# Five of the sixteen steps of L1F get other places in the schedule

## The chip, the cores and the metric

The kernel runs as one program on one core of a Trainium2 chip. The core has five engines, each with an instruction queue of its own that it works off in order: PE (matrix products), DVE (vector work), ACT (activation functions and copies), POOL (more vector work) and SP (issues DMAs). They meet only through semaphores. The metric is the time of the program on the device in microseconds (us).

## The reference

The network has four layers, L0 to L3. Each layer is a half-weighted feed-forward part, an attention and the same feed-forward part again, each applied to the layer-normed activations and added to them. `x` is 8 batches of 512 tokens by 128 features, f32. The change touches only L1's feed-forward part, called L1F here:

```
cluster_idx = argmax(calibrate(xf @ cluster_sigs.T))           # 8 clusters
tile_gates  = calibrate(xf @ sigs.T)                           # 64 tiles, 8 to a cluster
local_idx   = argmax(tile_gates of the chosen cluster)
comp = tanh(gelu(xf @ w1 + b1) @ w2 + b2)                      # 2 values a token
hh   = relu(comp @ spline_w1[tile] + spline_b1[tile])          # 16 values
mag  = hh @ spline_w2[tile] + spline_b2[tile]
y    = xf + mag * directions[tile] * output_scale
out  = layernorm(y) * gamma + beta
```

`calibrate` is a sigmoid, a place among 8 knots, a look-up of the knot's value and slope, and a line between them. L1's attention has 16 heads of 8 features over 512 tokens: scores, softmax, weighted sum, output product.

## The kernel before

`l0_block` does L0; `l0_tail` ends it and begins L1F; `l1_block` holds L1's attention with most of both L1F rounds beside it; `l2_block` and `l3_block` do the rest. What follows is about `l1_block`, which takes some 413 to 985 us of the profile.

**Units.** `l1_block` walks 128 units, (batch b, head group g, token tile i), 16 to a batch. In the text, u0 to u15 are the units of such a sixteen and block B is units 16B to 16B+15. Unit n issues, in two halves, `first(n)` (two matmuls a half, line 1290, into one of two PSUM buffers `s1`; then one DVE maximum over that buffer, line 1291, 128x2 out of 128x1024) and, 11 units late, `second(n-11)` (two matmuls a half, line 1310, with exponentials on ACT, line 1312). So PE can be at most one unit ahead of the maxima: the scores of a half wait for the maximum of the same half one unit before. After the two halves come the "works" planned for the unit, then, in every fourth unit, `weigh` (line 1320: 16 matmuls, 32 PE instructions), then the work of the dictionary `later`: the transposes `turn` (line 1330) with a reciprocal and a product on DVE (lines 1332, 1333), `back`, `leave`, and `maxima` (line 1298). With the lag of 11, `weigh` falls into u3, u7, u11 and u15. All PSUM tiles other than `s1` share one ring of four banks, `s2`: the scores of `second`, `o` of `weigh`, `tp` of `turn`, `pa`, `pp` and so on.

PE, ACT and DVE run in exactly the order in which the Python code issues (`manual_schedule`); POOL and SP are not in that list; the framework orders their instructions.

**The plan.** `todo` maps a slot to works; unit n carries out slots 2n and 2n+1. `plan` puts the steps of one L1F round of batch b at slots 32b + L1F_PLACES[k], for b = 2 to 7 and, for the second round, for two more with 32*8 and 32*9 in place of 32b:

```
L1F_PLACES = (-63, -58, -58, -55, -50, -50, -48, -47, -42, -42, -39, -37, -34, -31, -26, -22)
...
if b >= 2:
    self.plan(todo, [n + k for k in L1F_PLACES], *self.l1_ffn_steps(b, w, bank, room, self.xn[b], self.xt[b], aside=True))
```

Places repeat after 32 slots, so slot -63 is in u0, -58 in u3, -42 in u11, -31 in u0 of the next block, and so on. Eight rounds go through: their first halves (steps 1 to 13) lie in blocks 0 to 7, their last three steps one block later.

**The sixteen steps** (`l1_ffn_steps`):

```
steps = [lambda: powers(kept[:, :, 0:8]), places, lookup, gates, lambda: first("oc"), pick, lambda: powers(box["sg"]), places, lookup,
         gates, outer, turn, spline, direct, lambda: (whiten or self.whiten)(b, box["z"], box["z"]), update]
```

`powers` is one exponential on ACT (line 1081). `places` is five DVE operations on 128x32 (1087 to 1091). `lookup` is two DVE products of two SBUF operands (1096, 1097). `gates` is a DVE sum over the knots (1102) and two small DVE `tensor_tensor`, g (1104, 1105). `first` is five small DVE operations, the choice of a cluster (1111 to 1115). `pick` is a DVE product and a sum (1119, 1120). `outer` is a second choice and a product (1126). `turn` and `spline` go through PE, ACT and DVE (1131 to 1155). `direct` makes z on PE, ACT and POOL (1163, 1167). The norm, `whiten`, is four `bn_stats` on DVE (215), thirteen small POOL operations (219 to 236) and four POOL `tensor_scalar` (275). `update` is three POOL `tensor_tensor` on 128x512 (1173, 1175, 1176).

**What else is planned there.** For each next batch: a norm of x (`whiten`) at u7, its transposes on PE (line 314) at u9, the projections (1242, with rotation on POOL, 1246 and 1251) at u10 and u11, `values` at u12. In blocks 5 and 6 the front of a second L1F round comes on top (norm u15, transposes u2, scores and squeeze u3, its end u6). In block 7 the first steps of L2 take the place of the next batch's.

Of the kernel before, what the change touches and what calls it, by code (L numbers as in the profile page):

```python
# [70 lines left out]
values ffn1_13 squeeze6_1 clear11 ffn1_14 squeeze7_2 spread02 spread03 spread00 squeeze6_2 spread01  # L71
"""

L1F_PLACES = (-63, -58, -58, -55, -50, -50, -48, -47, -42, -42, -39, -37, -34, -31, -26, -22)
FIXED = {mybir.EngineType.PE, mybir.EngineType.Activation, mybir.EngineType.DVE}

ROWS = ["l0_bc", "l1_bo", "gamma", "beta", "l2_bo", "l3_bv"]
# [67 lines left out]
class Net:  # L145
# [1037 lines left out]
    def l1_block(self, w, w2, room, pool_w):  # L1183
# [18 lines left out]
        with ExitStack() as c:  # L1202
# [160 lines left out]
            for b in range(NB):  # L1363
# [5 lines left out]
                if b >= 2:  # L1369
                    self.plan(todo, [n + k for k in L1F_PLACES], *self.l1_ffn_steps(b, w, bank, room, self.xn[b], self.xt[b], aside=True))  # L1370
            for b in range(2):
                n = 32 * (NB + b)
                self.plan(todo, (n - 98, n - 91, n - 89, n - 89, n - 83), lambda _, b=b: self.whiten(b, self.xn[b]),
                          lambda xn, b=b: self.turned(xn, bank, self.xt[b]), *self.l1_ffn_front(b, w, bank, room))
                self.plan(todo, [n + k for k in L1F_PLACES], *self.l1_ffn_steps(b, w, bank, room, self.xn[b], self.xt[b], aside=True))
            n = 32 * NB - 50 + 32
# [713 lines left out]
```

## Time and profile before

| what | value |
|---|---|
| runs | 2604.12, 2608.65, 2613.46 us, median 2608.65 |
| the profiled execution | 2601.68 us, its span 2599.8 us |
| busy: PE, DVE, ACT, POOL | 91%, 78%, 68%, 44% of the span |
| granted PE clock, block 0 (417 to 484 us) | 0.75 |
| granted PE clock, blocks 1 to 6 (484 to 875 us) | 1.00 |
| length of blocks 0 to 7, us | 66.6, 63.8, 64.6, 64.5, 64.6, 67.2, 67.2, 59.1 |

The length of a block is the distance between the first line-1290 matmuls of its unit 0 and of the next block's. Within block 4, which starts at 676.53 us, the units last, from u0 to u15: 4.76, 2.45, 2.45, 5.77, 2.52, 3.72, 2.45, 5.77, 2.95, 4.18, 3.84, 7.41, 3.45, 4.00, 2.46, 6.41 us.

How to read the views: a timeline row gives the start, the time taken, the engine, the line of the code, the operation, output and inputs by the program's names, and how many instructions were merged (x6); in square brackets stands the idle time of the engine before it and who ended it. A row of the chain of waits gives start, length, engine, tile and line of the work that the end of the program was traced back through. In a group row, the numbers after the first bar are the time busy and the mean in ns of one instruction, after the second the idle time before them and what ended most of it.

### The profile page before, as it was taken

To read this page: it belongs to the slowest core of one execution; us is meant where nothing else is said; L and a number is where in the kernel's file an instruction comes from. 1 tells how busy PE (TensorE), PEld (TensorE's weight loads), DVE (VectorE), ACT (ScalarE), POOL (GpSimd) and SP (SyncE) were. 2 spreads that over 40 slices of the span, in tenths; PEclk is the share of its full clock that TensorE was granted. 3 is DMA by queue.
4 is the path that set the end of the run, shared out by engine and by line. 5 is a ranking of instruction groups with operands and counts; after the bars stand their busy time and mean duration, and the time that the engine had idled before them with its cause. 6 is when DMAs were issued, how large, how long until landed. Compare 5 with 4: busy or idle time off the path is not lost.

```text
span 2599.8 us, 51330 instructions
## 1 busy us (share of the span) xinstructions
PE 2375.4 (91%) x18184; PEld 1421.3 (55%) x18184; DVE 2019.7 (78%) x5582; ACT 1761.3 (68%) x4413; POOL 1154.4 (44%) x2016
## 2 busy tenths in 40 slices
PE   6868938999999998999999999999899999999997
PEld 6546623344444344565555655656565666666664
DVE  5356368888888847878878787876788989898897
ACT  2244233666677666866767667676688998999996
POOL 5754751444454332264352634432234545454443
PEclk9978957999999999999999999999899999999999
DMA  8221330001010100000000000000000000000000
GB/s 272 59 79 42 107 97 1 19 19 27 20 26 19 35 2 4 1 1 1 1 1 1 1 1 1 1 1 17 1 18 15 5 22 22 10 14 22 22 2 13
DMA packets 72976, 66.51 MB, mean 26 GB/s; under 512 B 15690, under 2 KB 62802, under 8 KB 70578
## 3 DMA queue, kind: packets, MB, share of 16 engines
q1 hardware_dynamic: 68112, 54.88, 7.8%
q0 software_dynamic: 3584, 7.58, 1.1%
q8 instruction: 145, 2.38, 0.4%
q10 hardware_dynamic: 1026, 0.78, 0.1%
q14 instruction: 109, 0.89, 0.1%
HBM read 36.47 MB, written 26.80 MB: 24 GB/s over the span
## 4 chain that ended last, share of the span: by engine, by line
PE 63%; DVE 21%; ACT 8%; POOL 4%; issue 2%; DMA 1%; SPq 0%; ACTq 0%; DVEq 0%; POOLq 0%
PE tp L1477 8%; PE s L1451 6%; PE s L1290 5%; PE o L1804 4%; PE o L1493 4%; PE o L1320 4%; PE s L1753 4%; PE yp L384 3%; PE s L1310 3%; ACT e L1760 3%; DVE nm L1291 3%; DVE nm L1455 3%; PE tp L1779 2%; PE pp L1721 2%; PE hp L684 2%
## 5 line engine op out<-in xcount | busy, mean ns | idle before, releaser
L1462 ACT ACTIVATE e<-s,nm 128x512 f32<-128x512 f32 x512 | 345.0, 688 | 25.9 <-DVE nm L1455 21.4
L1291 DVE TENSOR_REDUCE nm<-s 128x2 f32<-128x1024 f32 x256 | 301.3, 1218 | 75.8 <-PE s L1310 60.9
L1455 DVE TENSOR_REDUCE nm<-s 128x2 f32<-128x1024 f32 x256 | 300.9, 1216 | 29.8 <-PE s L1451 27.8
L1483 ACT ACTIVATE p<-tp 128x512 f32<-128x512 f32 x512 | 278.7, 617 | 63.8 <-PE tp L1477 63.8
L1312 ACT ACTIVATE pr<-s 128x512 f32<-128x512 f32 x512 | 271.5, 601 | 73.1 <-PE s L1310 69.5
L1477 PE MATMUL tp<-cst,e 128*128 128x128 f32 x2048 | 292.8, 281 | 15.2 <-DVE rs L1468 7.9
L1477 PEld LDWEIGHTS tp<-cst,e 128*128 128x128 f32 x2048 | 220.1, 141 | 153.7 <-issue 87.4
L1471 POOL TENSOR_SCALAR e<-e,rs 128x512 f32<-128x512 f32 x113 | 198.3, 1755 | 230.0 <-DVE rs L1468 191.5
L1290 PE MATMUL s<-k,q 32*128 32x512 f32 x1024 | 279.4, 658 | 18.0 <-DVE nm L1291 14.7
L1310 PE MATMUL s<-q,k 32*128 32x512 f32 x1024 | 290.3, 627 | 5.4 <-DVE at L1333 4.3
L1760 ACT ACTIVATE e<-e,m 128x512 f32<-128x512 f32 (+3 forms) x512 | 286.3, 571 | 12.7 <-DVE m L1757 12.5
L1757 DVE CUSTOM_DVE_ANT_0 e<-s,bias 128x512 f32<-128x512 f32 (+3 forms) x512 | 220.1, 486 | 93.2 <-PE s L1753 92.7
L219 POOL TENSOR_TENSOR d<-st 128x4 f32<-128x4 f32 (+3 forms) x90 | 19.5, 217 | 549.4 <-DVE st L215 351.3
L1781 ACT COPY pt<-tp 128x512 f32<-128x512 f32 x320 | 174.4, 589 | 90.3 <-PE tp L1779 90.2
L1471 DVE TENSOR_SCALAR e<-e,rs 128x512 f32<-128x512 f32 x399 | 195.6, 520 | 9.1
L1790 DVE TENSOR_SCALAR e<-e,rc 128x512 f32<-128x512 f32 (+3 forms) x512 | 190.0, 416 | 9.1
L386 DVE SCALAR_TENSOR_TENSOR x<-yp,sel,x 128x128 f32<-128x128 f32 x480 | 166.8, 348 | 32.4 <-PE yp L384 20.9
L1779 PE MATMUL tp<-cst,e 128*128 128x128 f32 x1280 | 171.0, 278 | 9.8 <-ACT pt L1781 4.0
L1451 PE MATMUL s<-k,q 32*128 32x512 f32 x1024 | 174.7, 651 | 5.1 <-ACT e L1462 2.6
L1753 PE MATMUL s<-qk 64*128 64x512 f32 (+3 forms) x1024 | 173.4, 457 | 2.0 <-DVE m L1757 1.3
L1493 PE MATMUL o<-p,va 128*32 128x128 f32 x4096 | 165.8, 277 | 2.9 <-ACT p L1483 2.9
L1779 PEld LDWEIGHTS tp<-cst,e 128*128 128x128 f32 x1280 | 139.2, 141 | 48.5 <-issue 13.6
(476 smaller groups left out, 4844.7 us busy)
## 6 DMA issues: line engine op xcount, KB each, us to landing
yd<-z SPq DMA_DIRECT2D x8, 1024.0 KB
r<-yd SPq DMA_DIRECT2D x32, 256.0 KB
sk<-pu SPq DMA_DIRECT2D x16, 256.0 KB
k<-sk SPq DMA_DIRECT2D x60, 64.0 KB
w<-in_l_w SPq DMA_DIRECT2D x14, 256.0 KB
xd<-wqkv SPq DMA_DIRECT2D x12, 256.0 KB
x<-in_x SPq DMA_DIRECT2D x8, 256.0 KB
up<-in_l_up SPq DMA_DIRECT2D x8, 256.0 KB
```

Of the source, the lines that this page charges most:

```text
L1290: nc.tensor.matmul(s[:, jj, :], lhsT=q[cut, g, i * P : (i + 1) * P], rhs=k[cut, g, :], start=True, stop=True)
L1291: nc.vector.tensor_reduce(nms[b, g // 2][:, i, 2 * h : 2 * h + 2, g % 2], s, AX.X, ALU.max, negate=True)
L1310: nc.tensor.matmul(s, lhsT=k[cut, g, kt * P : (kt + 1) * P], rhs=q[cut, g, :], start=True, stop=True)
L1451: nc.tensor.matmul(s[:, jj, :], lhsT=q[cut, g, i * P : (i + 1) * P], rhs=k[cut, g, :], start=True, stop=True)
L1455: nc.vector.tensor_reduce(nm, scores[n, h], AX.X, ALU.max, negate=True)
L1462: nc.scalar.activation(e, s[:, jj, :], AF.Exp, bias=nm[:, jj : jj + 1], accum_out=sm[:, jj : jj + 1])
L1471: (nc.gpsimd if h and jj and 14 <= n < last - 1 else nc.vector).tensor_scalar(e, e, rc[:, jj : jj + 1], None, ALU.mult)
L1477: nc.tensor.transpose(tp[:, kt, :], probs[n][j][:, kt * P : (kt + 1) * P], self.ident)
L1483: nc.scalar.activation(p, turns[n].pop(0), AF.Exp)
L1753: nc.tensor.matmul(s[:, jj, 0:w], lhsT=qs[n][cut, i * P : (i + 1) * P], rhs=ks[n][cut, 0:w], start=True, stop=True)
L1760: outs.append(lambda e=e, jj=jj: nc.scalar.activation(e, e, AF.Exp, bias=mins[n][:, jj, i : i + 1], scale=-1.0, accum_out=sums[n][:, jj, i ...
L1779: nc.tensor.transpose(tp[:, k, :], block(n, jj, i, kt), self.ident)
```

## The change

Only the tuple of places differs:

```diff
-L1F_PLACES = (-63, -58, -58, -55, -50, -50, -48, -47, -42, -42, -39, -37, -34, -31, -26, -22)
+L1F_PLACES = (-63, -61, -58, -55, -53, -51, -48, -47, -44, -42, -39, -37, -34, -31, -27, -22)
```

In units of a block this moves five steps:

| step | unit before | unit after |
|---|---|---|
| `places`, first round (step 2) | u3, ahead of `lookup` | u1 |
| `first("oc")` (step 5) | u7, ahead of `pick` | u5 |
| `pick` (step 6) | u7 | u6 |
| `lookup`, second round (step 9) | u11, ahead of `gates` | u10 |
| last norm, `whiten` of z (step 15) | u3, ahead of the next round's `places` | u2 |

No instruction is added or taken away, and L2's attention, which has a list of places of its own in `l2_block`, stays as it is. `places`, `first`, `pick` and `lookup` consist of DVE instructions alone; the norm is DVE and POOL.

## Prediction

> **What bounds the kernel.** I read the page's group list first. The maxima of L1's scores are the DVE's largest group there, and what ends the DVE's idle time before them is PE:
>
> ```profile
> L1291 DVE TENSOR_REDUCE nm<-s 128x2 f32<-128x1024 f32 x256 | 301.3, 1218 | 75.8 <-PE s L1310 60.9
> ```
>
> So in most places the DVE waits for PE. Next, the chain of waits through block 4 (676 to 742 us) shows where it is the other way round:
>
> ```profile
> 682.48 1.22 DVE nm L1291
> ...
> 688.47 3.57 PE o L1320 x32
> ...
> 695.50 0.54 DVE kd L1102
> ```
>
> The chain passes from PE to the maxima in u1 (682.48), is PE's alone in `weigh` (688.47 in u3, again at 702.93, 721.32 and 737.64), and in u4 goes through the DVE's `gates` (695.50). An ordinary unit is DVE-bound: PE needs 1.93 us for its scores (676.53 to 678.46 in u0), the two maxima need 2.42, the unit lasts 2.45. A `weigh` unit has 3.57 us more on PE, and DVE work planned there is under that cover. How much of the cover is used shows in the timeline of the DVE:
>
> ```profile
> 658.31 0.53 DVE L1104 TENSOR_TENSOR g<-t,kd 128x32 f32<-128x32 f32 x1
> 658.88 1.20 DVE L1105 TENSOR_TENSOR g<-g,kd 128x32 f32<-128x32 f32 x1
> ...
> 682.46 7.27 DVE L1291 TENSOR_REDUCE nm<-s 128x2 f32<-128x1024 f32 x6 [0.76 <-PE s L1310]
> ...
> 692.00 0.62 DVE L1097 TENSOR_TENSOR pr<-eq,tab 128x448 f32<-128x448 f32 x1
> 693.14 2.35 DVE L1291 TENSOR_REDUCE nm<-s 128x2 f32<-128x1024 f32 x2 [0.52 <-PE s L1310]
> ...
> 696.06 0.24 DVE L1104 TENSOR_TENSOR g<-t,kd 128x32 f32<-128x32 f32 x1
> ...
> 696.94 7.25 DVE L1291 TENSOR_REDUCE nm<-s 128x2 f32<-128x1024 f32 x6
> ```
>
> The six maxima of u1 to u3 run without a gap from 682.46 (the row's idle time of 0.76 is before the first). Norm, `places` and `lookup` follow, end at 692.62, and the DVE then still idles 0.52 us: in u3 all of them are free. From 696.94 the six of u5 to u7 run without a gap too, and the first two rows show the same two products g as at 696.06, but much longer. POOL's timeline says why:
>
> ```profile
> 657.51 2.52 POOL L1246 TENSOR_TENSOR rt<-rt,rope 128x512 f32<-128x512 f32 x2 [0.80 <-ACT rt L1245]
> ...
> 690.59 0.20 POOL L219 TENSOR_TENSOR d<-st 128x4 f32<-128x4 f32 x1 [8.38 <-DVE e L1087]
> ...
> 695.02 3.14 POOL L275 TENSOR_SCALAR z<-z,sm,rs 128x128 f32<-128x128 f32 x4
> 698.25 1.27 POOL L1173 TENSOR_TENSOR z<-z,gh 128x512 f32<-128x512 f32 x1
> ...
> 700.93 1.26 POOL L1176 TENSOR_TENSOR x<-x,z 128x512 f32<-128x512 f32 x1
> ```
>
> Beside a pair of POOL's 128x512 `tensor_tensor` (657.51 to 660.03) the g's took 0.53 and 1.20 us, each to about the end of one of the two. Beside POOL's `tensor_scalar` (695.02 to 698.16) they took 0.24 and 0.19. So the former block a DVE product of two SBUF tiles, the latter hardly do.
>
> **The change, part by part** (times of block 4; what is added to a unit's DVE queue always stands behind its own maxima and ahead of the next unit's, for which PE waits).
>
> *`places`, u3 to u1.* Five DVE operations, 1.13 us from the first's start to the next maximum (454.61 to 455.74 in block 0). In u1 they stand ahead of the maxima of u2; PE's u3 scores wait for those, and `weigh` is queued behind them: it began at 688.40, 1.10 after the last maximum of u2. Two pairs of maxima that no longer follow directly win a little back (six take 7.27, a spacing of 1.21; a pair alone 2.36, a spacing of 1.14): 1.13 - 2 x 0.07 = **1.0 us late**. Nothing returns in u3, whose DVE queue had already been free. In blocks 5 and 6 PE's own transposes (750.55) lengthen u2 to 2.79 and take 0.3 of it: 0.7.
>
> *The last norm, u3 to u2.* Its 0.78 us on the DVE (689.64 to 690.42) now stand ahead of u3's maxima. PE's next use of those is u4, behind `weigh`'s 3.57 us: nothing. z has been there since 682.20. But POOL starts earlier, and here is a new wait. u2's maxima end at 688.3, `bn_stats` at 689.1, and POOL's run begins at 689.15. From its begin to the first 128x512 operation it took 7.66 us in this block (690.59 to 698.25) and 7.07 with nothing beside it (741.17 to 748.24, an earlier part of block 5). So POOL's three-operation `update` starts at 696.2 to 697.0 and lasts 4 us; before, it lay under the maxima of u5 and u6, which read PSUM (their 1.21 is unchanged there). u4's maxima start at 693.14 + 1.0, `gates` 2.27 later, its g's at 697.05: inside POOL's first operation. Each waits for one POOL operation's end, at 697.5 to 698.3 and 698.85 to 699.6, where they would have ended at 697.5. That is 1.3 to 2.1, and 1.7 is the middle; the rows at 658.31 and 658.88 cost 1.3 in the same situation, by 0.29 and 1.01. Bounds: 0 if POOL misses them altogether, 2.4 if both wait for a whole 1.26 less their slack. I take **1.7 us**, the worked-out position. Behind the g's stand u4's `at` (line 1333), for which PE already waits in u5 (a bank of `s2`: matmul at 697.17, idle 0.38), and u5's maxima, so all of it is late.
>
> The Trainium skill weighs here, in "SBUF — State Buffer", section "Who interferes with whom": a DVE instruction with two SBUF inputs blocks against any GpSimd instruction that reads SBUF. By it the `tensor_scalar` at 695.02 would have held the g's too, some 1.3 us that the profile does not show (0.24 and 0.19); the move would then cost only about 0.4 a block here, and the whole sum would be about 14 us. I go by the rows.
>
> *`first`, u7 to u5.* 1.11 us (704.89 to 706.00) ahead of u6's maxima, less 0.14 as above: u5 to u7 are DVE-bound, `weigh` of u7 comes **1.0 late**. *`pick`, u7 to u6.* 1.03 us ahead of u7's maxima, covered by `weigh` as the norm was. What is late next: the norm of x in u7 now stands behind `pick` instead of before both, so relative to PE POOL starts it 0.9 later; its last tile came at 712.25, the last transpose of it at 713.36, a slack of 1.1. Just covered: nothing, but 0.5 to 0.9 in six blocks if POOL is slower.
>
> *Second `lookup`, u11 to u10.* 1.35 us (720.85 to 722.27 less a gap) go into 1.49 us of idle DVE before u11's maxima (716 to 718.58). In u11 `gates` ends up to 2.8 earlier, clear of POOL's rotation, but the DVE idled 1.30 before the maxima of u12 already, waiting for PE behind `weigh`. Nothing in blocks 1 to 7.
>
> *Two blocks differ.* In block 0 PE runs no `second` until u11; u6 and u7 begin with DVE idle times of 1.04 and 1.05, which take `first` and `pick`, and u9 waits for POOL either way (457.66). In u11, though, the maxima at 469.82 start straight behind a 1.19 us g; without it PE is ready at about 467.7 to 468.6. I put down **-1.3** (0 to -2). In block 7 the transposes of u9 wait for POOL (tile at 913.25, transpose at 913.31; u9 lasts 5.25 against 4.0 to 4.2), and there `first` and `pick` had stood ahead of the norm; the same wait shrinks by **1.2**. After unit 128 there are no maxima, and the norm's move is off the path.
>
> **Sum.** Blocks 1 to 4: 4 x (1.0 + 1.7 + 1.0) = 14.8. Blocks 5 and 6: 2 x (0.7 + 1.7 + 1.0) = 6.8. Block 7: 3.7 - 1.2 = 2.5. Block 0: -1.3. Together +22.8 us, all between 417 and 935 us. Against the profiled execution (2601.68, of which 2599.8 span) that is 2624.5; it was 7 us quicker than the median of the runs, 2608.65, and measured times are medians, so I forecast 2608.65 + 22.8 = **2631.5 us**.
>
> **The rivals.** (1) POOL's `update` misses `gates`: 7 x 1.7 less, +10.9, 2619.5. For it: a POOL run 0.4 longer than worked out lets the first g through. Against: then the second g, or `first` at about 700.3, meets the rest of its 4 us. (2) The x norm comes too late for u9, or both g's pay 2.4: 5 us each, up to +33, 2641.5. For it: a slack of 0.2 after the shift; against: in blocks 5 and 6 the slack was 1.6. (3) Faster: POOL's hold on the g's of u11 sets the start of u12. Moving `lookup` frees the DVE 2.8 us sooner there, and if u12's maxima had waited for it they would gain what block 0 gains, 1.3 in each of eight blocks; with `places` and `first` absorbed by the 0.5 us that PE is idle in a bare unit this gives -10, 2598. It decides from the point where the DVE's end in u11 is later than PE's scores of u12. Against: the DVE had 1.30 to spare. (4) The path does not move: PE's gaps of 0.46 and 0.18 in u2 and u3 take the shifts, 2608.65. Against: the gaps are waits for the very maxima that come later.
>
> **Numbers.** Forecast 0.57, rival 1 0.21, rival 2 0.11, rival 3 0.06, rival 4 0.05. About 0.3%, 7.8 us, is what a measurement here can tell from no change. Faster 0.06; within it 0.07 (rival 4 and the lower edge of rival 1); slower 0.87. The range, 2614 to 2642, spans rivals 1 and 2 with some microseconds of spread between runs (2604 to 2613 before), and leaves out the faster case and no change.
>
> **What would show it.** Block 4 should last 68.3 us instead of 64.6; u3's `weigh` begins 1.0 later within its block; the DVE's g's in u4 take around 0.5 to 1.2 each; u6 and u7 show `first` and `pick` between maxima; the DVE idles some 2 us in u3 and u7 before the next maxima, unused cover. If u4's g's stay at 0.2, rival 1 holds. If blocks 1 to 4 are no longer than before, the reading of the cover is wrong.

## The result, and the profile after

Medians of six runs each: 2608.73 us before (2604.12 to 2613.46), 2623.39 us after (2620.27 to 2630.36). The ratio is 1.0063, 95% interval 1.0051 to 1.0076: 13.3 to 19.8 us slower, 14.7 by the medians. The profiled execution took 2627.5 us, of which 2625.5 span.

| length, us | 0 | 1 | 2 | 3 | 4 | 5 | 6 | 7 | sum |
|---|---|---|---|---|---|---|---|---|---|
| blocks before | 66.63 | 63.79 | 64.61 | 64.46 | 64.61 | 67.15 | 67.17 | 59.09 | 517.5 |
| blocks after | 65.24 | 67.79 | 66.95 | 66.82 | 67.44 | 71.39 | 70.28 | 60.86 | 536.8 |
| difference | -1.39 | +4.00 | +2.34 | +2.36 | +2.83 | +4.24 | +3.11 | +1.77 | +19.3 |

Block 7 is counted here to the first scores of its u15. The profile shows 25.8 us more for the whole execution, 19.3 of it in the blocks. The rest is 0.3 before L1, 5.9 between the last score of L1 (line 1290) and the first of L2 (line 1753), and 0.3 after that. The 5.9 are a matter of their own, further below. The profiled execution of before was 7 us quicker than its median and this one 4 us slower, so the profiles differ by more than the medians.

The group of the maxima is as busy as it was (301.3 us) and the DVE's idle time before it grew from 75.8 to 101.8 us. The moved work left its old places empty:

```profile
L1291 DVE TENSOR_REDUCE nm<-s 128x2 f32<-128x1024 f32 x256 | 301.3, 1217 | 101.8 <-PE s L1310 88.9
```

The chain of waits in block 4 (from 684.11 us on), which answers to the chain shown of before:

```profile
696.99 3.57 PE o L1320 x32
...
704.02 0.54 DVE kd L1102
704.58 0.77 DVE g L1104
706.20 1.09 PE s L1310 x2
```

u3's `weigh` now starts 12.88 us into the block (696.99) where it started 11.94 into it (688.47). New on the chain is the product g (704.58). Behind it on the DVE stands `at` (line 1333), for which PE waits with the scores of `second` (706.20; idle 0.89 where it had been 0.38). The DVE's timeline of the same stretch says what happened in each unit:

```profile
692.32 0.17 DVE L1087 TENSOR_SCALAR e<-e 128x32 f32<-128x32 f32 x1
...
693.45 2.35 DVE L1291 TENSOR_REDUCE nm<-s 128x2 f32<-128x1024 f32 x2
...
701.67 2.35 DVE L1291 TENSOR_REDUCE nm<-s 128x2 f32<-128x1024 f32 x2 [1.88 <-PE s L1310]
...
704.58 0.76 DVE L1104 TENSOR_TENSOR g<-t,kd 128x32 f32<-128x32 f32 x1
705.37 0.19 DVE L1105 TENSOR_TENSOR g<-g,kd 128x32 f32<-128x32 f32 x1
...
718.08 2.35 DVE L1291 TENSOR_REDUCE nm<-s 128x2 f32<-128x1024 f32 x2 [1.85 <-PE s L1310]
```

`places` (from 692.32) pushes the maxima of u2 back to 693.45, by 1.13. In u3 and u7 the DVE now idles 1.88 and 1.85 us under `weigh`: unused cover. Of the two g's the first is held (0.76 where it had been 0.24) and the second is not (0.19). POOL's timeline has the holder:

```profile
700.80 3.14 POOL L275 TENSOR_SCALAR z<-z,sm,rs 128x128 f32<-128x128 f32 x4
704.02 1.27 POOL L1173 TENSOR_TENSOR z<-z,gh 128x512 f32<-128x512 f32 x1
705.37 1.32 POOL L1175 TENSOR_TENSOR z<-z,gh 128x512 f32<-128x512 f32 x1
```

The first g ends at 705.34, POOL's first operation at 705.29. The second g runs at the boundary to POOL's next, which starts at 705.37 and takes 1.32 in place of 1.27. So it was in blocks 2, 3, 4 and 7, and in block 6, where the first g took 1.03. In blocks 1 and 5 the second g was held too and took 1.30, and u5 is 1.1 longer there than in the neighbours (5.34 against 4.23, 4.87 against 3.75).

### The profile page after: what moved, and what is told of

Read it like the earlier page. It is cut to its first block, busy times and chain, and to the rows that moved or that the text cites. A ratio compares the mean times of both kernels' runs of the same rounds, so it can differ in the third digit from the quotient of the medians.

```text
span 2625.5 us, 51330 instructions
## 1 busy us (share of the span) xinstructions
PE 2382.8 (91%) x18184; PEld 1421.6 (54%) x18184; DVE 2014.3 (77%) x5582; ACT 1760.8 (67%) x4413; POOL 1154.8 (44%) x2016
## 4 chain that ended last, share of the span: by engine, by line
PE 62%; DVE 22%; ACT 8%; POOL 4%; issue 2%; DMA 1%; SPq 0%; ACTq 0%; DVEq 0%; POOLq 0%
PE tp L1477 8%; PE s L1451 6%; PE s L1290 5%; PE o L1320 4%; PE o L1493 4%; PE o L1804 4%; DVE nm L1291 4%; PE s L1753 4%; PE yp L384 3%; PE s L1310 3%; ACT e L1760 3%; DVE nm L1455 3%; PE tp L1779 2%; PE pp L1721 2%; PE hp L684 2%
## 5 line engine op out<-in xcount | busy, mean ns | idle before, releaser
L1291 DVE TENSOR_REDUCE nm<-s 128x2 f32<-128x1024 f32 x256 | 301.3, 1217 | 101.8 <-PE s L1310 88.9
L1483 ACT ACTIVATE p<-tp 128x512 f32<-128x512 f32 x512 | 278.7, 617 | 62.8 <-PE tp L1477 62.8
L1310 PE MATMUL s<-q,k 32*128 32x512 f32 x1024 | 296.3, 641 | 11.0 <-DVE at L1333 9.3
L1477 PEld LDWEIGHTS tp<-cst,e 128*128 128x128 f32 x2048 | 220.1, 141 | 152.9 <-issue 87.4
L1760 ACT ACTIVATE e<-e,m 128x512 f32<-128x512 f32 (+3 forms) x512 | 286.2, 570 | 13.3 <-DVE m L1757 13.1
L1290 PEld LDWEIGHTS s<-k,q 32*128 32x128 f32 x1024 | 90.0, 195 | 145.6 <-DVE nm L1291 101.5
```

Of the source, the lines that this page charges most:

```text
L1290: nc.tensor.matmul(s[:, jj, :], lhsT=q[cut, g, i * P : (i + 1) * P], rhs=k[cut, g, :], start=True, stop=True)
L1291: nc.vector.tensor_reduce(nms[b, g // 2][:, i, 2 * h : 2 * h + 2, g % 2], s, AX.X, ALU.max, negate=True)
L1310: nc.tensor.matmul(s, lhsT=k[cut, g, kt * P : (kt + 1) * P], rhs=q[cut, g, :], start=True, stop=True)
L1477: nc.tensor.transpose(tp[:, kt, :], probs[n][j][:, kt * P : (kt + 1) * P], self.ident)
L1483: nc.scalar.activation(p, turns[n].pop(0), AF.Exp)
L1760: outs.append(lambda e=e, jj=jj: nc.scalar.activation(e, e, AF.Exp, bias=mins[n][:, jj, i : i + 1], scale=-1.0, accum_out=sums[n][:, jj, i ...
```

## The experiments

The theory is the prediction's: whatever is taken out from under `weigh` and put ahead of bare maxima is late by its own time, and POOL's `update` holds any two-input product of the DVE that it meets. The rivals: that only the g's waits count, that gates' new waits or the x norm are the whole cost, or that u11's look-up earns something in every block. Each kernel was timed beside the kernel before on the same chip. That took 2640 us on the chips of the first two sets (e1 to e7 and the change again; L1 starts at 445 to 452 us there) and 2608 on that of the last (e8 to e10), so the ratios are what compares. A half-clock stretch is one in which the profile shows a granted PE clock of 0.50; "clean" is a unit or block without one. "Bare" is a unit without `weigh` or other long work of PE.

| kernel | ratio to before | 95% interval | clean block 3 or 4, us |
|---|---|---|---|
| before | 1 | | 64.5 |
| `places` alone | 1.0028 | 1.0014 to 1.0043 | 65.4 |
| norm alone | 1.0064 | 1.0043 to 1.0086 | 65.5 (block 2) |
| `first` alone | 1.0085 | 1.0060 to 1.0110 | none clean |
| second look-up alone | 1.0000 | 0.9981 to 1.0020 | 64.5 |
| norm and `first` | 1.0046 | 1.0031 to 1.0061 | 66.1 |
| the change | 1.0063 | 1.0051 to 1.0076 | 66.8 |
| the change again | 1.0067 | 1.0040 to 1.0094 | 66.8 |
| the change with the norm put back | 1.0123 | 1.0108 to 1.0138 | 68.3 |
| second `places` to u10 | 1.0001 | 0.9985 to 1.0017 | 64.3 |
| first gates to u3 | 0.9987 | 0.9975 to 0.9999 | 63.4 |
| gates, second `places`, second look-up | 0.9972 | 0.9962 to 0.9983 | 62.8 |
| gates, second look-up, `outer` | 0.9961 | 0.9948 to 0.9974 | 62.6 |

### One part at a time

**`places` alone** (step 2):

```diff
-L1F_PLACES = (-63, -58, -58, -55, -50, ...
+L1F_PLACES = (-63, -61, -58, -55, -50, ...
```

> Only the first `places` moves, u3 to u1. Theory (the uncovered DVE time is the cost): u2 lasts 3.4 us instead of 2.45, u3 stays at 5.8, so 0.95 in each of blocks 1 to 4 and 7 and 0.6 in blocks 5 and 6: +6 us. POOL's run is where it was relative to u3's norm, so the g's of u4 stay at 0.2. Rival (most of the measured loss is POOL holding the g's and PE's clock dropping): no loss from this step, 0 to +1 us.

2645.32 us against 2639.81, as expected. u2 lasts 3.40 in place of 2.45 (3.47 in place of 2.79 in blocks 5 and 6), and the other clean units of blocks 2 to 6 are what they were, within 0.15. The g's stay at 0.24 or 0.25 and 0.19 (0.19 and 0.19 in blocks 5 and 6) although POOL's `tensor_scalar` run beside them.

**The norm alone** (step 15):

```diff
-..., -34, -31, -26, -22)
+..., -34, -31, -27, -22)
```

> Only the last norm moves, u3 to u2. Theory: its own 0.78 us on the DVE are covered by the weigh of u3, so u3 keeps its length; what it costs is POOL's update meeting the g's of u4, 0.5 us in each block from 1 to 7 as in the changed kernel (one g held, the other slipping through), up to 1.3 where both are held: +3 to +9 us. Rival (a norm ahead of u3's maxima is as uncovered as places): 0.8 more in u3 of seven blocks, +9 to +14 us. Rival (all of it is covered): 0.

2657.44 us, above what was expected. u2 and u3 are unchanged (2.46, 5.77), so the norm itself costs nothing in u2. u5 lasts 4.55 in place of 3.72. The DVE's timeline of block 4 has it in the first g:

```profile
730.94 1.07 DVE L1104 TENSOR_TENSOR g<-t,kd 128x32 f32<-128x32 f32 x1
```

It was held for 0.83, by POOL's first operation of `update` (730.69 to 731.95); the second, at 732.04, took its 0.19. In block 5 the second was held too (1.30). u6 or u7 are longer too in blocks 1, 3, 4 and 5 (in block 4 3.51 and 6.14 in place of 2.45 and 5.77), where half-clock stretches follow PE's wait; blocks 1 to 6 are 10.9 us longer in all. In block 4 the knock-on, 1.4 us in u6 and u7, costs more than the 0.83 of the hold.

**`first("oc")` alone** (step 5, beside an unmoved `pick`):

```diff
-..., -55, -50, -50, -48, ...
+..., -55, -53, -50, -48, ...
```

> Only `first` moves, u7 to u5; `pick` stays in u7. Theory: u6 lasts 3.25 us instead of 2.45, 0.8 in each of blocks 1 to 6; nothing in block 0 (idle DVE) and nothing in block 7 (the norm that u9 waits for comes that much earlier): +4.8 us, and g's of u4 at 0.2. Rival (the DVE work only shifts inside a stretch that weigh ends anyway): 0.

A miss, far above what was expected: 2661.16 us. u6 lasts 5.24, 2.79 more, in blocks 1 to 4 and 7 (4.33 and 4.24 in blocks 5 and 6). The DVE's timeline of block 2, behind u5's maxima, shows two of the five operations of `first` held:

```profile
605.51 1.28 DVE L1113 TENSOR_TENSOR r<-r,cst 128x32 f32<-128x32 f32 x1
606.82 0.19 DVE L1114 TENSOR_REDUCE fm<-r 128x4 f32<-128x32 f32 x1
607.04 1.08 DVE L1115 TENSOR_TENSOR oc<-r,fm 128x32 f32<-128x32 f32 x1
```

and POOL's timeline what they waited for:

```profile
604.12 1.27 POOL L1173 TENSOR_TENSOR z<-z,gh 128x512 f32<-128x512 f32 x1
605.47 1.27 POOL L1175 TENSOR_TENSOR z<-z,gh 128x512 f32<-128x512 f32 x1
606.82 1.26 POOL L1176 TENSOR_TENSOR x<-x,z 128x512 f32<-128x512 f32 x1
```

With the norm where it was, `update` lies under u5's end and u6, harmless as long as only maxima of PSUM run there. `first` puts two-input products into it, and 1.09 (line 1113) and 0.89 (line 1115) come on top of its own 1.1. PE then idles 2.96 us before u7's scores (609.31) and runs at half clock from 610.10 to 613.50.

**The second look-up alone** (step 9):

```diff
-..., -48, -47, -42, -42, ...
+..., -48, -47, -44, -42, ...
```

> Only the second `lookup` moves, u11 to u10. Theory: block 0 loses 1.3 us (u12's maxima no longer wait for a held g), blocks 1 to 7 stay within 0.2 of their length: -1.4 us in the profile, too little for the times to tell. Rival (the freed 2.8 us of DVE in u11 shorten u12 everywhere): -1.3 in each of eight blocks, -10 us.

2639.54 us. u12 and u13 of block 0 fall from 4.54 and 3.72 to 3.92 and 3.30. In blocks 1 to 6 the g's of u11 take 0.30 (0.19 in block 6) and 0.19 in place of 0.54 and 1.20, and no clean unit behind them is shorter: the DVE was early there anyway.

### Together

**The norm and `first`:**

```diff
-..., -55, -50, -50, ..., -31, -26, -22)
+..., -55, -53, -50, ..., -31, -27, -22)
```

> The norm goes to u2 and `first` to u5; `places`, `pick` and `lookup` stay. Theory (POOL's update holds whatever DVE products meet it: `first` in u5 alone met it and paid 2.8 us; with the norm in u2 the update starts about 2 us earlier, meets the g's of u4 and is over when `first` comes): u5 lasts 4.2 to 4.6 instead of 3.72, u6 3.25 instead of 5.24, together +1.6 us a block, +10 to +12 us, 0.4%, below `first` alone (+0.85%) though one more step is moved. Rival (the costs of the two moves add): +0.64% and +0.85% make +1.5%, +39 us.

2652.38 us against 2639.64: less slow than `first` alone, though one step more is moved (the two intervals just touch, at 1.006; the lengths of the units show it more plainly). (Beside the norm alone the intervals overlap; its clean block is 0.6 longer.) u5 lasts 4.55, u6 3.26 in place of 5.24. The norm's move shifts `update` forward, out of `first` and into the g's.

**The change again** (no edit), beside these:

> The changed kernel once more, on the chip of the experiments. Theory: blocks 2 and 3 last 66.9 us as in its first profile, about 2.4 more than before (u2 0.95, u5 0.5, u6 0.8), and the ratio is 1.006. The 6 us by which the end of the stage (from the last score matmul of `first` to L2's first scores) was longer in its first profile, 56.3 against 50.3, were stretches of half PE clock in work that the change leaves alone; if they are chance, this profile has other ones there. Rival (they belong to the change): 56 us again.

2660.10 us against 2639.64; its clean units have the lengths that they had on the first chip, but for u5 of block 5, where the second g was not held this time (3.76 for 4.87). Half-clock stretches stand in blocks 1, 2 and 4 again, and one in block 6. From L1's last scores to L2's first it is 56.2 again, as the rival had it.

**The change with the norm put back,** that is, with one moved step less:

```diff
-L1F_PLACES = (-63, -61, -58, -55, -53, -51, -48, -47, -44, -42, -39, -37, -34, -31, -27, -22)
+L1F_PLACES = (-63, -61, -58, -55, -53, -51, -48, -47, -44, -42, -39, -37, -34, -31, -26, -22)
```

> The changed kernel with the norm put back into u3; `places`, `first`, `pick` and `lookup` stay moved. Theory (POOL's update holds whatever DVE products of two SBUF tiles it meets): the update starts at the begin of u6 as in the kernel before, meets `first` behind u5's maxima and holds it as in `first` alone; the g's of u4 are free. u2 3.4, u5 3.7, u6 5.2 us: 2.1 to 2.8 more than before plus places' 0.95, minus block 0: slower than the changed kernel, 1.009 to 1.011. Rival (the norm's move costs about 0.5 a block, as u5 of the changed kernel seems to say): faster than the changed kernel, 1.005.

2638.90 us against 2608.32, twice the loss of the change and a little above the expected 1.009 to 1.011. The DVE's timeline of block 4, with the g's free and `first` held:

```profile
714.35 0.22 DVE L1104 TENSOR_TENSOR g<-t,kd 128x32 f32<-128x32 f32 x1
...
717.91 1.27 DVE L1113 TENSOR_TENSOR r<-r,cst 128x32 f32<-128x32 f32 x1
...
719.44 1.08 DVE L1115 TENSOR_TENSOR oc<-r,fm 128x32 f32<-128x32 f32 x1
```

The one clean block lasts 68.3, 1.4 more than the change's 66.8; there are half-clock stretches in blocks 1, 2, 3, 5 and 6. So within the change the norm's move is no cost but a gain.

### The other way: more work under `weigh`

**The second `places` from u8 to u10** (step 8), where the DVE idles before u11's maxima:

```diff
-..., -48, -47, -42, -42, ...
+..., -48, -44, -42, -42, ...
```

> Another layout: the kernel before, with only the second `places` moved from u8 to u10, into the 1.5 us of idle DVE ahead of u11's maxima. Theory (DVE work is free where weigh or the projections cover it and costs its length where it does not): u9 lasts 3.1 to 3.4 us instead of 4.0 to 4.2, bounded by POOL's norm of x, in blocks 1 to 6, nothing in blocks 0 and 7, u10 and u11 as before: -5 us, 0.998. Rival (u9 is bound by POOL anyway, or the rotation on POOL holds u10's DVE work): 0.

A miss: 2637.55 against 2639.64, no difference. u9 is 0.85 to 1.0 shorter (3.17), but u13 lasts 4.62 in place of 4.00. The DVE's timeline of block 4 shows why: this late, the chain of the second round runs into POOL's rotation (749.17 to 758.13).

```profile
749.28 1.20 DVE L1089 TENSOR_SCALAR f<-f 128x32 f32<-128x32 f32 x1
...
754.12 1.27 DVE L1096 TENSOR_TENSOR eq<-y,cst 128x224 f32<-128x224 f32 x1
755.42 1.58 DVE L1097 TENSOR_TENSOR pr<-eq,tab 128x448 f32<-128x448 f32 x1
```

The two products of `lookup` take 1.27 and 1.58 where they took 0.73 and 0.62, the maxima of u12 start later, and the 1.30 us for which the DVE had idled before them are gone. A clean block still gains 0.2; what takes it back is u12 of block 0 (6.45 in place of 4.54) and half-clock stretches in blocks 2 and 4, which are 1.0 and 1.1 longer than before.

**The first `gates` from u4 to u3** (steps 1, 2 and 4; `places` then lies in u15 of the block before; `max` puts what would come before the first unit into it):

```diff
-L1F_PLACES = (-63, -58, -58, -55, ...
+L1F_PLACES = (-68, -66, -58, -57, ...
...
-                    self.plan(todo, [n + k for k in L1F_PLACES], ...
+                    self.plan(todo, [max(n + k, 1) for k in L1F_PLACES], ...
```

> Another layout: the first `powers` and `places` go to u14 and u15 of the block before (behind `spline`, under weigh), and the first `gates` from u4 to u3, in the room that `places` leaves. Theory: u4 has only the reciprocal and product of `turn` behind its maxima, u5 lasts 2.5 to 2.7 instead of 3.72, u3, u15 and u7 keep their length: -1.0 us in each of blocks 1 to 7, -7 us, 0.997. Rival (u5 waits for something else, or u15's cover is too short: DVE idle 2.0 us there in blocks 1 to 4, 1.25 in 5 and 6): 0 or slower.

2636.69 against 2639.64, less than half of the gain expected. u5 lasts 2.69 in place of 3.72 in blocks 1 to 4 and 7. In blocks 5 and 6 a half-clock stretch in u10 (5.24 and 5.06 in place of 3.84) takes more than that, and the block is 1.3 longer.

**Steps 8 and 9 both into u10, on top of that:**

```diff
-L1F_PLACES = (-68, -66, -58, -57, -50, -50, -48, -47, -42, -42, ...
+L1F_PLACES = (-68, -66, -58, -57, -50, -50, -48, -44, -44, -42, ...
```

> The layout with `gates` in u3, and besides the second `places` and the second `lookup` both in u10, under the cover of the projections and weigh of u11. Theory: u5 2.7 us (1.0 less than before), u9 3.2 (0.9 less) in blocks 1 to 6; the DVE ends in u11 before u12's scores come, so that u13 keeps 4.0 us, which it did not where only the second `places` was moved (4.62): -1.0 in seven blocks, -0.9 in six, about -12 us, 0.9955. Rival (the rotation on POOL holds the products in u10 and u11 for longer than the cover): u12 and u13 take back 0.6 to 1, 0.998.

2601.28 against 2608.32, a ratio between the expectation's 0.9955 and its rival's 0.998. u9 keeps its gain (3.20) and u13, with the look-up in u10 as well, gives back only 0.24 to 0.25.

**The look-up to u10 and `outer` to u11** (steps 9 and 11), with step 8 where it was:

```diff
-L1F_PLACES = (-68, -66, -58, -57, -50, -50, -48, -47, -42, -42, -39, ...
+L1F_PLACES = (-68, -66, -58, -57, -50, -50, -48, -47, -44, -42, -41, ...
```

> The layout with `gates` in u3, the second `lookup` in u10 and `outer` in u11 instead of u12. Theory: u5 2.7 us; block 0 1.4 shorter; `outer` (1.46 us) leaves u12 but its products meet POOL's rotation in u11 and end about 0.6 us after u12's scores are there, so u12 and u13 together lose 0.5 to 0.9: -1.0 and -0.7 in seven blocks, -1.4 in block 0, -13 us, 0.995. Rival (the rotation holds three products for 1.26 each): u12 starts its maxima late, nothing gained over the layout with `gates` in u3, 0.9985.

2597.77 (2593.32 to 2599.26) against 2608.32: 10.5 us faster than before and, by the two ratios, some 27 faster than the change. The DVE's timeline of block 4 has `gates` in u3, in the cover that the change left empty,

```profile
689.28 0.19 DVE L1105 TENSOR_TENSOR g<-g,kd 128x32 f32<-128x32 f32 x1
690.03 2.35 DVE L1291 TENSOR_REDUCE nm<-s 128x2 f32<-128x1024 f32 x2 [0.55 <-PE s L1310]
```

and, in another part of it, `outer` in u11, held by the rotation and yet free:

```profile
718.65 0.94 DVE L1115 TENSOR_TENSOR ol<-r,fm 128x32 f32<-128x32 f32 x1
719.62 1.43 DVE L1126 TENSOR_TENSOR sel<-oc,ol 128x256 f32<-128x256 f32 x1
721.69 2.36 DVE L1291 TENSOR_REDUCE nm<-s 128x2 f32<-128x1024 f32 x2 [0.64 <-PE s L1310]
```

Two products lose time (0.94 and 1.43 for 0.19 and 0.42), but the DVE still idles 0.64 before the maxima at 721.69. u5 lasts 2.69 and u13 2.94; a block of 64.5 lasts 62.6.

## Why the prediction was right, and where its steps were not

The time came within the range, 8 us below the forecast, and by the mechanism named: work moved from under `weigh` to bare units is late by about its own length. It lies nearer to rival 1's 2619.5, whose sign (u4's g's at 0.2) the profile shows for the second g only, in five blocks of seven. Some of the agreement is luck: of the 19.3 us in the blocks about 3.3 come from two things that the sum did not have, `pick` in blocks 5 and 6 and half-clock stretches in blocks 1, 2 and 4; its own terms make some 16 where it had 22.8. Term by term, in clean units (of blocks 2 and 3 where no other block is named):

| term | forecast | measured | where |
|---|---|---|---|
| `places` in u1 | 1.0 | 0.95 | u2, 2.45 to 3.40; alone 0.95 |
| `places`, blocks 5 and 6 | 0.7 | 0.64 | u2, 2.79 to 3.43; alone 0.68 |
| norm: u4's g's held | 1.7 | 0.5 | u5, 3.72 to 4.23 (block 6: 0.8) |
| `first` in u5 | 1.0 | 0.8 | u6, 2.45 to 3.26 |
| `pick`, blocks 1 to 4 | 0 | 0 | u7, 5.77 in block 3 |
| `pick`, blocks 5 and 6 | 0 | 0.97 | u7, 6.49 to 7.46 |
| block 0 | -1.3 | -1.4 | 1.1 of it in u12 and u13 |
| block 7 | 2.5 | 1.8 | u9's wait gone, 5.25 to 4.12; a half-clock stretch each, before and after |

**The mis-sized term** is "I take 1.7 us, the worked-out position". POOL came where the step put it (its `update` begins 19.91 us into block 4, worked out for 19.7 to 20.5), and the first g paid 0.52, near the 0.5 that the position implies. What failed is "Each waits for one POOL operation's end": the second g waited in 2 of 7 blocks only, although in the row it was taken from (658.88) it did. In the four profiles with the norm in u2 (the change twice, the norm alone, the norm and `first`) there are 28 such meetings, in which the second g and POOL's next operation start within 0.02 us of each other. In 22 the g takes 0.19 and POOL's operation 1.32 or 1.33, in 6 the g takes 1.30 or 1.31 and POOL's operation 1.26 or 1.27: it looks as if one went first and the other waited for it. Block 1 of the change is among the 6 both times, block 5 in one of the two profiles; which comes first can't be read from the record, and the prediction had no ground for either. The Trainium skill, in "SBUF — State Buffer", section "Who interferes with whom", states that the pair of ports which DVE and GpSimd (POOL here) share is an exclusive lock. The 28 meetings agree with it. Its other sentence, by which POOL's `tensor_scalar` would hold the g's too, is not seen in the kernel with `places` alone (0.25 and 0.19 in block 4, beside a `tensor_scalar`). That u5's 0.5 is near the 0.4 that the prediction worked out from that sentence is therefore no support for it.

**The terms were added, and they don't add.** The three parts alone cost 0.28, 0.64 and 0.85%, the change 0.63%. The norm alone costs, and with `first` moved it saves, since `update` has to hold either the g's (0.5 to 0.8) or `first` (2.0). The prediction had the fact in hand. Rival 1 says "Against: then the second g, or `first` at about 700.3, meets the rest of its 4 us", but prices that rival at +10.9, as if a missed hold were a gain. With the norm put back, where `update` does miss the g's, the loss doubles.

**`pick` was "covered by `weigh`"** only where nothing else stood in u6. In blocks 5 and 6 the end of the second round's front stands there. The DVE's timeline of block 5:

```profile
781.87 0.61 DVE L1120 TENSOR_REDUCE sg<-sel 128x32 f32<-128x256 f32 x1
782.40 0.41 DVE L1060 TENSOR_TENSOR cm<-ht,cw 128x256 f32<-128x256 f32 x1
782.85 0.42 DVE L1061 TENSOR_REDUCE cp<-cm 128x8 f32<-128x256 f32 x1
```

ACT's timeline shows who waits for line 1061:

```profile
783.30 0.49 ACT L1063 ACTIVATE comp<-cp,cb 128x4 f32<-128x4 f32 x2 [2.69 <-DVE cp L1061]
783.70 2.03 ACT L1312 ACTIVATE pr<-s 128x512 f32<-128x512 f32 x4
```

ACT works in order, so the exponentials pr of u7 stand behind that tanh (its idle time was 0.92 before), and `weigh` stands behind them: PE idles 1.62 before it in place of 0.65. A clean u7 lasts 7.46 in the kernels with `pick` in u6 (the change, both times) and 6.49 with it in u7 (the parts alone, and the norm with `first`). That the second round's front ends in u6 was in the list of what is planned there; the prediction did not follow `pick` to it.

**The slack of the x norm** held: u9 lasts 4.10 to 4.12 in blocks 1 to 4, where it was 4.02 to 4.18. Rival 2 did not occur, but for the doubly held g's in blocks 1 and 5. Rival 3 is excluded by the look-up alone, rival 4 by u2.

**Not foreseen at all** were half-clock stretches. The windows view of the change's block 4 (start and end, length, then busy time of PE, PE's loads, DVE, ACT and POOL with instruction counts, granted PE clock):

```profile
703.99:707.40 3.41, 2.52 (x17) 0.86 (x16) 3.31 (x8) 1.75 (x4) 3.22 (x3) 1.00 0.00 0
707.40:710.80 3.40, 3.40 (x20) 1.21 (x24) 2.95 (x7) 1.61 (x3) 0.63 (x1) 0.50 0.00 0
```

After 3.41 us in which PE idled 0.89, it ran 3.40 us at half clock, and u6 and u7 last 3.47 and 6.19 where clean ones last 3.26 and 5.77: 0.63 us. Blocks 1 to 6 of before have none; the change has them in blocks 1, 2 and 4, at 506.0, 574.3 and 707.4. With `first` alone they add 1.2 to 2.7 us to u7 (6.93 to 8.43 in place of 5.77 in blocks 1 to 4), beside the 2.0 by which `update` holds `first`.

Their places lie on a grid. In each of the 13 profiles the half-clock stretches of L1 and up to L2 start whole multiples of 3.413 us apart (in the change's, 506.0, 574.3, 707.4 and 949.7 are 20, 39 and 71 such steps apart). Whether a wait of PE leads to one can depend on how it falls on this grid. `first` alone in block 2 and the norm put back in block 4 have the same wait of 2.96 us before u7's scores. In the former most of it lies in one step of the grid, which shows PE busy for 0.79 of 3.40:

```profile
606.70:610.10 3.40, 0.79 (x8) 0.31 (x8) 3.33 (x5) 0.81 (x2) 1.30 (x2) 1.00 0.00 0
610.10:613.50 3.40, 3.40 (x20) 0.90 (x20) 2.45 (x3) 1.98 (x4) 0.00 (x0) 0.50 0.00 0
```

In the latter it is split between two steps (PE busy 2.05 of 716.70 to 720.10 and 1.79 of 720.10 to 723.50), the clock stays at 1.00, and u7 lasts 5.77. Busy time in a step does not decide alone: a stretch followed 2.52 busy of 3.41 in the change (703.99), none followed 1.78 of 3.40 (782.50). What else decides is open. The Trainium skill, in "TensorE: Matmul & The Clock Gate", section "Part 1: The HAM clock gate (the "warmup" mystery)", gives a free-running window of 3413 ns and a halved clock after an idle one. The grid agrees; a window idle only for 0.89 of 3.41 is less than that asks for.

**The 5.9 us between L1 and L2** are of the same kind. Before, the stretch from L1's last scores on is

```profile
934.60:986.60 52.00, 48.02 (x286) 20.71 (x286) 11.94 (x30) 31.24 (x63) 13.31 (x22) 1.00 0.02 6
```

and after

```profile
954.10:1012.00 57.90, 53.94 (x284) 22.61 (x284) 11.95 (x30) 31.51 (x63) 13.31 (x22) 0.88 0.02 5
...
966.80:970.20 3.40, 3.40 (x15) 1.79 (x14) 0.20 (x2) 3.40 (x8) 2.73 (x11) 1.00 0.02 5
970.20:977.00 6.80, 6.80 (x30) 1.68 (x30) 0.00 (x0) 2.31 (x5) 6.28 (x10) 0.50 0.01 2
```

The same instructions, and PE is busy 5.9 longer at a granted clock of 0.88. It isn't bound to the moved steps: from the last line-1290 matmul to L2's first score it is 50.3 before and in the profiles of the look-up alone and of the second `places` alone, 52.3 and 53.1 with `places` alone and the norm put back, and 55.9 to 56.3 in all others, the three kernels faster than before among them. The lengths go with the half-clock stretches in between: none where it is 50.3, 5.7 us of them with `places` alone, 6.8 with the norm put back, and twice 6.8 in the eight others. And these go with the grid. From L1's last score matmul to the next step of the grid it is 3.1 to 3.3 us in the three profiles without a stretch, 2.2 with `places` alone, 1.1 with the norm put back, and 0.3 to 0.8 in the eight. So in these profiles the length goes with where L1's end falls on the grid, whatever was moved. What stays open is whether a kernel's other executions fall on the grid as the profiled one did; the two profiles of the change, on two chips, have 0.8 and 0.7. As the medians differ by 14.7, less than the blocks alone, the profiled execution of before, 7 us quicker than its median, may be a favourable one.

## What to carry to other kernels

In this kernel side work cost nothing under a long unit of the binding engine (here `weigh`), or in the unit ahead of it where the queue runs ahead, as long as no other engine held it or waited for it, and nearly its full length ahead of a bare one; a schedule that spread the work evenly over units was therefore worse than one that heaped it where the cover is. Before adding the costs of several moves, lay their new places on one time line with the other vector engine's operations: two moves can take each other's collision away or make it. Before a few microseconds are put down to an edit, see whether half-clock stretches moved with it. A step "covered" by the long unit must also be followed to the other engines that wait for what is queued behind it.

## What the runs showed of the hardware

- POOL's 128x512 `tensor_tensor` held small DVE products of two SBUF tiles to its end (0.19 to as much as 1.30), and in u10 of the kernel with the second `places` moved (block 4) also `tensor_scalar` of one input (1.20 and 1.19 for 0.18). POOL's 128x128 `tensor_scalar` did not hold the g's (0.24, 0.19). Maxima over PSUM kept their 1.21 to 1.23, `tensor_reduce` over SBUF its 0.19 (606.82 in `first` alone).
- At the boundary between two such POOL operations a waiting DVE product slips in or waits another whole operation: 0.19 in five blocks, 1.30 in two, in one execution; 22 and 6 in four. Where it slips in, POOL's operation takes 1.32 or 1.33 in place of 1.26 or 1.27.
- Half-clock stretches of 3.4 and 6.8 us appear in mid-kernel on a grid of 3.413 us, after grid steps in which PE idled 0.8 us (631.6 with the second `places` moved, 2.60 of 3.40 busy) to 2.8, but not after each such step (1.62 idle at 782.5 in the change). Between L1 and L2 they appear also where PE's row is full (966.80 to 970.20 shows 3.40 of 3.40 busy ahead of one, with 15 matmuls where the full steps from 700.58 and 963.40 have 28 and 25, so the row may hide idle time).
